# Comparing hot source numbers by tensor_tensor with a broadcast PSUM column in a gated graph layer

## The chip, the cores and the metric

The kernel runs on one core of a Trainium2 chip. The metric is the time of one execution in microseconds (us) on the device. Before the change the median of three runs is 2913.64 us (2913.59 to 2916.97).

The engines have short names here, as in the profile: PE is the matrix engine (PEld its weight load), DVE the vector engine, ACT the scalar engine, POOL is GpSimd, SP the engine that here only issues DMAs. SBUF is the on-chip memory, PSUM the smaller one that PE writes its results to.

## The reference

There are 12,500 nodes with 128 features each and 412,500 edges, sorted by their destination. Cut to what matters:

```python
theta = x[dst] - x[src]
w = sigmoid(relu(theta @ W1 + b1) @ W2 + b2)       # one gate for each edge
agg = segment_sum(w * theta, dst)
indeg = segment_sum(ones, dst)
x = layernorm(x + agg + indeg * (x @ W4 + b4))
```

So for each edge the row of its source is needed twice: through W1 for the gate, and as it is for the sum.

## The kernel before

**Tiles and stages.** First comes an opening (about 300 us): it writes a table `z` to DRAM that holds `x @ W1` and `x` for each node, keeps 8,192 of the nodes' rows in SBUF as three bfloat16 terms (`tabs`), and works on the first 18 parts of the edge list with simpler code (`early_part`). Then `part(s)` (line 1508) runs for s = 18, 19 and so on, 258 times with work of its own; two parts make a block of 104 destination nodes. Each part takes up to 1,532 edges in two kinds. Up to 1,024 *cold* edges have their source rows fetched from `z` by indirect DMA: POOL issues eight of these a part, 128 rows each (`gather`, line 404), into one of five buffers `zbuf`. Up to 512 *hot* edges have their rows picked out of `tabs` by a matrix product instead: the sources lie in 32 ranges of 256 nodes, and for each range a part has 16 hot places.

**The hot tiles.** For four ranges and up to eight parts at once, `hot_load` (line 1034) copies the hot places' source numbers, each counted from the start of its range, into `hot_src`, the same 512 half-precision numbers in every partition. `hot_tiles` (line 1046) makes two bfloat16 one-hot tiles `of` from them: partition p and tile t stand for node 2p + t of the range, and `nodes[:, t:t+1]` holds that number, so each tile is one compare on DVE (line 1052). One such fetch, two compares, falls to each part. A part later `hot_products` multiplies the tiles with `tabs` on PE (line 1068), and `hot_out` copies the rows out (line 1082, ACT). There are two `of` buffers in turn, counted by `turn_of`. In the opening five groups of such fetches (`OPENING`, line 55) fill the pipeline, 16 compares of 64 to 512 columns. Behind them 514 compares follow, 512 columns wide but for the last ones.

**What a part does on each engine.** The order on PE, DVE and ACT is written out by hand: within `part` each engine does its work in the order of the code. On DVE a part is:

- `logits` (lines 964 to 975): subtract the gathered rows from the destinations' rows `y` (964, needs the gathers), multiply (969), compare for the destination tile (939), sum up (975)
- in every other part `finish` (1237) and in the others `one_hot_h` (1154)
- `fetch_step`, which makes the two compares of line 1052
- `spend`, which does steps of placing (below)
- in every other part `normalize` (1265 to 1290)

PE in a part does the hot products with W1 (1118, 1119), then the destinations' rows of the part after next (900, into a PSUM buffer that line 964 must have read), then the hot logits (1132), the turning of hot rows (1135), and the sums of the block mixed with the products of line 1068. ACT makes one-hot tiles (879, 880), gates and scales rows (988, 1006, 1141, 1144), and copies.

**Placing.** The edge list is prepared for 64 parts at a time by the generator `place` (line 503): for each range it takes the eight largest keys, strikes them out, and flips a bit field, on DVE, with 767 columns each (lines 593, 596 and 588, with 590 in the first set). `spend` (line 1380) takes such steps as long as a part's credit lasts, 2.5 a part. So DVE has stretches with placing, in which it does these steps beside each part, and stretches without. In line 588 the other operand is a column of the PSUM tile `fix` that is broadcast along the row (`steps_c`, line 302). The tile `fix` also holds `iota_f` and `w2_b`, which lines 939, 1154 and 969 read.

**The lines that the change touches.** `fix` is carved up in lines 299 to 302; `constants` (line 324) fills the constant tiles, among them `nodes` (line 346); `hot_tiles` is in lines 1046 to 1053.

Of the kernel before, what the change touches and what calls it, by code (L numbers as in the profile page):

```python
# [14 lines left out]
AF = mybir.ActivationFunctionType  # L15
OP = mybir.AluOpType
# [4 lines left out]
P = 128  # L21
D = 128
# [4 lines left out]
WB = 104  # L27
# [19 lines left out]
HT = 2  # L47
# [7 lines left out]
OPENING = ((0,), (1, 7), (2, 6), (3, 5), (4,))  # L55
NU = 4
# [28 lines left out]
def gnn_resnorm(  # L85
# [37 lines left out]
    nc = tc.nc  # L123
# [16 lines left out]
    while n0 < N:  # L140
        t = max(1, (N - n0) // P)
# [157 lines left out]
    fix = cps.tile([P, 512], F32, name="fix")  # L299
    iota_f = fix[:, :WB].rearrange("p (o m) -> p o m", o=1)  # L300
    w2_b = fix[:, WB:WB + D]
    steps_c = fix.bitcast(I32)[:, WB + D:WB + D + HR.bit_length() - 1]
    w2_f = w2_r.rearrange("p (o m) -> p o m", o=1)

    oh_all = const.tile([P, NO * RW], F32, name="oh")
# [18 lines left out]
    def constants():  # L324

        nc.vector.tensor_copy(ident_b, ident)
        nc.vector.tensor_scalar_mul(nident_b, ident, -1.0)
        nc.vector.tensor_scalar_mul(wneg, wts[:, 0, :], -1.0)
        nc.scalar.activation(fix[:, :WB], iota_row[:, :WB], AF.Copy)

        nc.scalar.activation(w2_b, w2_r, AF.Copy)
        for k in range(HR.bit_length() - 1):
            nc.vector.memset(steps_c[:, k:k + 1], ((2 << k) - 1) << FIELD)
        half = const.tile([P, 1], F32, name="half")
        nc.vector.tensor_scalar(half, iota_p, float(HALF), -float(HALF), op0=OP.is_ge, op1=OP.mult)
        nc.vector.tensor_add(half, half, iota_p)
        nc.vector.tensor_scalar(mine, half, float(SW), None, op0=OP.is_lt)
        nc.vector.tensor_scalar(away, half, float(SW), -2.0, op0=OP.is_gt, op1=OP.mult)
        nc.vector.tensor_mul(half, half, mine)
        nc.vector.tensor_sub(away, away, half)  # L340
        nc.vector.tensor_scalar_mul(less, mine, -1.0)

        nodes = const.tile([P, HT], F32, name="nodes")
        node_c = const.tile([P, 1], F32, name="node_c")
        nc.vector.tensor_scalar(node_c, iota_p, float(HT), None, op0=OP.mult)
        nc.vector.tensor_scalar(nodes, iota_row[:, :HT], node_c, None, op0=OP.add)

        most = const.tile([P, 1], F32, name="most")
        nc.vector.memset(most, float(SW + HKL))
        apart = const.tile([P, PM], F32, name="apart")  # L350
        nc.vector.tensor_scalar(apart, iota_row[:, :PM], float(HOT), None, op0=OP.mult)
        return nodes, (apart, most)
# [14 lines left out]
    hot_src = const.tile([P, NU, RG * HB * HS], F16, name="hot_src")  # L367
# [358 lines left out]
    with tc.manual_schedule(engines={SP}), tc.tile_pool(name="work", bufs=2) as wp, tc.tile_pool(  # L726
# [312 lines left out]
        turn_of = [0]  # L1039

        def hot_of(i, x, w):

            of = of_half[i].rearrange("p (t e) -> p t e", t=HT)
            return of[:, :, x:x + w]

        def hot_tiles(f, x=0):

            i0, g, i1, i = f
            w = (i1 - i0) * HS * RG
            of = hot_of(turn_of[0] % 2, x, w)  # L1050
            for t in range(HT):
                nc.vector.tensor_scalar(of[:, t, :], hot_src[:, i % NU, :w], nodes[:, t:t + 1], None,
                                        op0=OP.is_equal)

        def hot_products(f, x, pd, steps_of):

# [264 lines left out]
        with after(done[1]):  # L1321
            place_first_dst(0, FIRST, ps_l, dst_f)
            nodes, hot_c = constants()
            start_of(0, FIRST)
# [20 lines left out]
        def tiles_of(group):  # L1345

            x = 0
            for f in group:
                hot_tiles(f, x)
                tiled.append((f, x))  # L1350
                x += (f[2] - f[0]) * EP
# [108 lines left out]
        groups, firsts, i = [], {}, 0  # L1460
# [311 lines left out]
```

## Time and profile before

| | |
|---|---|
| profiled execution | 2916.98 us |
| its span, first to last instruction | 2915.2 us |
| granted clock of PE, mean | 0.94 |
| PE busy | 2539.6 us (87%) |
| DVE busy | 2409.2 us (83%) |
| ACT busy | 2167.7 us (74%) |
| POOL busy | 2134.1 us (73%) |
| compares of line 1052 | 530, of them 502 with 512 columns |

An engine's busy time is the time in which it executes something; waiting and issuing are not counted. The page names groups by line, engine, operation, and tiles (written, then read). An entry of the waits has the engine and line that waited, what ended the wait, the total in us, how many times, and the longest. A window's row has its bounds, its length, and then the busy time and number of instructions of each engine, the granted clock, and the DMA engines' share and GB/s.

### The profile page before, as it was taken

The numbers are of one execution on the slowest core, as the hardware profiler recorded it, in microseconds if no ns is written. First come the engines' busy times: TensorE is split into PE (matmuls) and PEld (weight loads), VectorE is DVE, ScalarE is ACT, GpSimd is POOL, SyncE is SP. The second block draws the span as 40 slices with busy tenths as digits, with TensorE's granted clock in tenths as the row PEclk, the third lists the DMA queues.
The fourth block names the chain that finished last, engine by engine and source line by source line (L and its number), as shares of the span: only waits on it lengthen the run. The fifth ranks groups of instructions, "written<-read, shape, count | busy, mean of one in ns | idle before, by whom it ended". The sixth has DMA issues, their size and how long they took to land.

```text
span 2915.2 us, 59242 instructions
## 1 busy us (share of the span) xinstructions
PE 2539.6 (87%) x18606; PEld 2005.0 (69%) x18606; DVE 2409.2 (83%) x4413; ACT 2167.7 (74%) x6556; POOL 2134.1 (73%) x2213
## 2 busy tenths in 40 slices
PE   6867899999988999888888889888988899888996
PEld 6646677777776777676766667666776777666775
DVE  7888699998967999988558989988567999888664
ACT  6489877777877778677777767776776877677776
POOL 4556777777777777777777777777777777777774
PEclk8787999999999999999999999999999999999998
DMA  8544555455554555455554555555554555545542
GB/s 276 164 140 130 146 140 137 139 142 140 140 150 133 141 143 140 136 143 136 141 153 132 140 136 143 138 136 140 137 141 134 138 137 143 139 135 142 140 137 76
DMA packets 239330, 413.59 MB, mean 142 GB/s; under 512 B 63423, under 2 KB 147226, under 8 KB 237470
## 3 DMA queue, kind: packets, MB, share of 16 engines
q0 software_dynamic: 105280, 286.93, 35.4%
q1 hardware_dynamic: 131756, 116.40, 15.0%
q10 hardware_dynamic: 1970, 6.40, 0.6%
q8 instruction: 148, 2.42, 0.3%
q14 instruction: 176, 1.44, 0.2%
HBM read 388.57 MB, written 20.94 MB: 140 GB/s over the span
## 4 chain that ended last, share of the span: by engine, by line
PE 39%; ACT 22%; DVE 20%; DMA 10%; issue 8%; POOL 1%; DVEq 0%; ACTq 0%; SPq 0%; POOLq 0%
PE pa L1171 13%; DMA zbuf<-z,src_i 9%; DVE zbuf L964 6%; PE y L900 5%; PE pd L1068 5%; ACT wx L1006 4%; PE px L1132 4%; ACT wxh L1144 3%; PE pz L1118 3%; PE pz L1119 3%; PE pz L1135 3%; ACT oh L879 2%; ACT oh L880 2%; ACT xT L1082 2%; DVE ed L593 1%
## 5 line engine op out<-in xcount | busy, mean ns | idle before, releaser
L404 POOL DMA_INDIRECT zbuf<-z,src_i x2060 | 1991.3, 967 | 634.1 <-issue 247.1
L1006 ACT ACTIVATE wx<-zbuf,wx 128x128 f32<-128x128 f32 x2060 | 630.3, 388 | 0.0
L1171 PE MATMUL pa<-wx,ow 128*104 128x260 f32 (+1 forms) x2284 | 622.5, 390 | 0.0
L900 PEld LDWEIGHTS y<-y,oh 128*128 128x128 f32 (+1 forms) x2156 | 277.7, 198 | 403.1 <-DVE zbuf L964 357.5
L1068 PEld LDWEIGHTS <-tabs 128*128 128x128 bf16 x6360 | 448.9, 100 | 121.8 <-issue 5.9
L1068 PE MATMUL pd<-of,tabs 128*128 128x128 bf16 (+3 forms) x6360 | 530.7, 222 | 0.0
L1124 ACT ACTIVATE hr<-pz 128x512 f32<-128x512 f32 x258 | 152.9, 593 | 495.1 <-PE pz L1119 494.8
L900 PE MATMUL y<-y,oh 128*128 128x128 f32 (+1 forms) x2156 | 314.3, 291 | 214.1 <-DVE zbuf L964 205.3
L964 DVE TENSOR_TENSOR zbuf<-y,zbuf 128x1024 f32<-128x1024 f32 x258 | 314.9, 1220 | 166.2 <-DMA zbuf<-z,src_i 164.6
L1171 PEld LDWEIGHTS pa<-wx,ow 128*104 128x104 f32 x2284 | 338.2, 177 | 40.8
L975 DVE TENSOR_REDUCE lg<-zbuf 128x8 f32<-128x1024 f32 x273 | 329.8, 1208 | 14.1 <-ACT oh L879 0.5
L969 DVE SCALAR_TENSOR_TENSOR zbuf<-zbuf,fix 128x1024 f32<-128x1024 f32 x273 | 331.5, 1215 | 9.3
L1171 PE MATMUL pa<-wxh,owh 128*104 128x130 f32 x2064 | 326.9, 295 | 0.0
L1144 ACT ACTIVATE wxh<-pz,wxh 128x128 f32<-128x128 f32 x1032 | 294.4, 368 | 40.4 <-PE pz L1135 34.4
L1118 PE MATMUL pz<-xT,wni 128*128 128x512 f32 x516 | 279.4, 623 | 3.8 <-ACT wxh L1144 3.8
L1171 PEld LDWEIGHTS pa<-wxh,owh 128*104 128x104 f32 x2064 | 272.1, 185 | 0.0
L1132 PEld LDWEIGHTS px<-w_c,hr 128*128 128x128 f32 x2064 | 264.1, 200 | 9.9 <-ACT hr L1124 9.9
L1132 PE MATMUL px<-w_c,hr 128*128 128x1 f32 x2064 | 263.5, 249 | 7.1 <-ACT hr L1124 7.1
L1119 PE MATMUL pz<-oh,y 128*128 128x512 f32 x516 | 265.4, 596 | 1.0 <-ACT oh L880 1.0
L879 ACT ACTIVATE oh<-to_all,away,mine 128x512 f32<-128x512 bf16 (+1 forms) x257 | 213.6, 831 | 3.1 <-DMA to_all<-off_d 3.1
L1119 PEld LDWEIGHTS pz<-oh,y 128*128 128x128 f32 x516 | 98.6, 191 | 125.5 <-issue 123.7
L1135 PE MATMUL pz<-wni,xT 128*128 128x128 f32 x1032 | 176.0, 297 | 0.0
(308 smaller groups left out, 3675.9 us busy)
## 6 DMA issues: line engine op xcount, KB each, us to landing
to_all<-off_d SPq DMA_DIRECT2D x258, 128.0 KB
zbuf<-z,src_i POOLq DMA_INDIRECT x2060
hot_src<-hot_s SPq DMA_DIRECT2D x228, 128.0 KB
y<-z SPq DMA_DIRECT2D x270, 28.0 KB
xw<-in_x_dram SPq DMA_DIRECT2D x138, 52.0 KB
out_dram<-o SPq DMA_DIRECT2D x138, 52.0 KB
wx<-in_x_dram ACTq DMA_DIRECT2D x12, 512.0 KB
z<-zbuf SPq DMA_DIRECT2D x6, 1024.0 KB
```

The lines of the kernel that those rows point to most:

```text
L404: ins = nc.gpsimd.indirect_dma_start(out=rows_of(s)[:, k, :], out_offset=None, in_=z if s >= NH else x, in_offset=IndirectOffsetOnAxis(ap= ...
L900: nc.tensor.matmul(y[:, j, :], d["oh"][:, (k0 + j) * P:(k0 + j + 1) * P], y_of(s), start=True, stop=True)
L964: nc.vector.tensor_sub(half, yy.to_broadcast([P, 2, n, D]), half)
L969: nc.vector.scalar_tensor_tensor(h[:, at, :], h[:, at, :], 0.0, w2.to_broadcast([P, n, D]), op0=OP.max, op1=OP.mult)
L975: nc.vector.tensor_reduce(lg[:, at, 0], h[:, at, :], AX.X, OP.add)
L1006: weighed[0] = nc.scalar.activation(wx[:, k, :D], rows_of(s)[:, k, D:], AF.Copy, scale=wx[:, k, D:D + 1])
L1068: steps_of.append(lambda q=q, i=i, t=t, j=j: nc.tensor.matmul(to[:, q], tabs[:, g, i, q, t, :], of[:, t, q], start=j == 0, stop=j == HT * ...
L1118: nc.tensor.matmul(pz, wneg, xT, start=True, stop=False)
L1119: nc.tensor.matmul(pz, y_of(t), blocks[t // SUB]["oh"][:, BP:], start=False, stop=True)
L1132: nc.tensor.matmul(lgh()[:, t % SUB, q:q + 1], hr[:, at], w2_c, start=True, stop=True)
L1144: nc.scalar.activation(wx[:, q, :D], pz[:, q * P:(q + 1) * P], AF.Copy, scale=wx[:, q, D:D + 1])
L1171: return [lambda i=i, one=one, w=w: nc.tensor.matmul(to if len(w.shape) == 3 else to[:, 0, :], one, w, start=first and i == 0, stop=last a ...
```

## The change

A new name `nodes_c` is given to two free columns of the PSUM tile `fix`, and ACT copies `nodes` there once in the opening. In `hot_tiles` the compares of the five opening groups stay as they were: `tensor_scalar` with the node number as a per-partition scalar from SBUF. All later ones become `tensor_tensor` on DVE: the first operand is the node number's PSUM column (32-bit floats), broadcast along the row, and the second is `hot_src` (half precision, SBUF). Output and values are the same.

```diff
@@ gnn_resnorm @@
     steps_c = fix.bitcast(I32)[:, WB + D:WB + D + HR.bit_length() - 1]
+    nodes_c = fix[:, WB + D + 8:WB + D + 8 + HT]
     w2_f = w2_r.rearrange("p (o m) -> p o m", o=1)
@@ constants @@
         nc.vector.tensor_scalar(nodes, iota_row[:, :HT], node_c, None, op0=OP.add)
+        nc.scalar.activation(nodes_c, nodes, AF.Copy)
@@ hot_tiles @@
             for t in range(HT):
-                nc.vector.tensor_scalar(of[:, t, :], hot_src[:, i % NU, :w], nodes[:, t:t + 1], None,
-                                        op0=OP.is_equal)
+                if turn_of[0] < len(OPENING):
+                    nc.vector.tensor_scalar(of[:, t, :], hot_src[:, i % NU, :w], nodes[:, t:t + 1], None,
+                                            op0=OP.is_equal)
+                else:
+                    nc.vector.tensor_tensor(of[:, t, :], nodes_c[:, t:t + 1].to_broadcast([P, w]),
+                                            hot_src[:, i % NU, :w], op=OP.is_equal)
```

## The prediction

> **What bounds the kernel now.** I first read the waits over the whole run, to see who sets the pace.
>
> ```profile
> DVE zbuf L964 <- DMA zbuf<-z,src_i: 164.6, 78, 5.8
> POOL zbuf L404 <- ACT wx L1006: 141.4, 464, 0.3
> DVE px L1265 <- ACT px L1247: 90.4, 43, 5.5
> DVE a L1237 <- ACT xuT L827: 76.0, 31, 6.3
> PEld y L900 <- DVE zbuf L964: 357.5, 200, 9.7
> L404 POOL DMA_INDIRECT zbuf<-z,src_i x2060 | 1991.3, 967 | 634.1 <-issue 247.1 <-ACT wx L1006 141.4 <-DMA zbuf<-z,src_i 49.4
> L404 POOL DMA_INDIRECT zbuf<-z,src_i x2060: 940/946/1782, 269.3 to 2886.9; - x188
> ```
>
> DVE's longest total wait is for gathers (first row). POOL, which issues them, is kept by nobody: its waits, whoever is named, are never over 0.3 us. A gather takes 0.967 us, and 634.1 / 2060 = 0.308 us lie ahead of it, so 1.275 us each and 10.2 us for the eight of a part. From 269.3 to 2886.9 us POOL does nothing but this. In the long run a part cannot be shorter.
>
> But DVE is nearly full beside it, in places. The next view gives busy times of all engines; I put the bounds where stretches with placing steps begin and end, as DVE's share shows them.
>
> ```profile
> core 0: us, PE busy (x) PEld busy (x) DVE busy (x) ACT busy (x) POOL busy (x), PEclk, DMA share, GB/s
> 298.00:387.00 89.00, 74.69 (x578) 60.31 (x577) 63.04 (x120) 71.29 (x218) 67.98 (x70) 0.94 0.49 137
> 387.00:700.00 313.00, 285.41 (x2142) 225.39 (x2141) 294.90 (x512) 236.62 (x732) 238.04 (x247) 0.97 0.51 140
> 700.00:855.00 155.00, 140.65 (x1090) 111.47 (x1089) 131.56 (x240) 124.11 (x382) 117.63 (x123) 0.99 0.51 141
> 943.00:1340.00 397.00, 357.06 (x2669) 281.33 (x2668) 368.79 (x652) 300.36 (x929) 301.88 (x313) 0.96 0.51 140
> 1340.00:1502.00 162.00, 145.12 (x1099) 114.39 (x1098) 106.10 (x179) 122.44 (x377) 122.80 (x129) 0.97 0.51 140
> 1588.00:1992.00 404.00, 359.32 (x2688) 281.10 (x2686) 369.76 (x655) 300.61 (x930) 307.23 (x318) 0.97 0.51 139
> 1992.00:2157.00 165.00, 147.41 (x1082) 116.24 (x1080) 106.18 (x177) 119.62 (x373) 125.39 (x131) 0.95 0.51 139
> 2157.00:2246.00 89.00, 74.86 (x535) 61.38 (x535) 64.11 (x124) 64.38 (x197) 67.67 (x71) 0.88 0.49 134
> 2246.00:2644.00 398.00, 356.22 (x2687) 278.67 (x2686) 369.88 (x659) 300.36 (x928) 302.94 (x313) 0.97 0.52 139
> 2644.00:2840.00 196.00, 178.91 (x1300) 143.08 (x1299) 127.87 (x210) 144.13 (x445) 148.47 (x157) 0.92 0.52 140
> ```
>
> Three kinds of stretch are to be seen. In the four with placing (from 387, 943, 1588 and 2246) DVE is busy 1403.3 of 1512 us, 93%. In the light ones (from 1340, 1992, 2644) it has a third of its time free. In the four short ones between (from 298, 855, 1502, 2157; the first and last are shown) a new set is started. POOL's rate is the same in all, 0.79 gathers per us, so the heavy stretches sit where two engines are full, POOL and DVE, and PE is at 90%.
>
> **The change part by part.** *The price of a compare.* What stands now, and the nearest forms of what comes:
>
> ```profile
> L1052 DVE TENSOR_SCALAR of<-hot_src,nodes 128x512 bf16<-128x512 f16 x502 | 161.8, 364 | 6.0 <-PE pd L1068 3.1 <-DMA hot_src<-hot_s 2.9
> L939 DVE TENSOR_TENSOR ow<-fix,rel 128x416 f32<-128x416 f32 x265 | 153.8, 581 | 0.0
> L1154 DVE TENSOR_TENSOR owh<-fix,hrel 128x832 f32<-128x832 f32 x129 | 130.7, 1013 | 0.0
> L588 DVE TENSOR_TENSOR ew<-ew,fix 128x767 int32<-128x767 int32 x124 | 117.8, 950 | 2.6
> L961 DVE TENSOR_TENSOR zbuf<-y,zbuf 128x512 f32<-128x512 f32 x19 | 12.6, 682 | 3.2 <-PE y L900 3.1
> ```
>
> Lines 939 and 1154 are is_equal compares of a PSUM operand with an SBUF operand of 16 bits (`rel`, `hrel`). Between them (1013 - 581) / 416 = 1.04 ns are paid for each column, so 581 + 96 x 1.04 = 681 ns for 512 columns. Line 588, with a broadcast PSUM column as here, has 767 columns at 950 where this line gives 946; line 961 has just 512 columns at 682. All agree, so I take 681 - 364 = 317 ns more for each compare. Its bounds are 300 and 340, since neighbours overlap by some tens of ns. [...]
>
> *In the heavy stretches.* Their compares (the third has 80, too), and what DVE waited for there, for the first and the last of the four:
>
> ```profile
> 387.00:700.00 313.00, 20.62 (x64) 0.97 0.51 140
> 943.00:1340.00 397.00, 25.62 (x80) 0.96 0.51 140
> ...
> 2246.00:2644.00 398.00, 25.59 (x80) 0.97 0.52 139
> DVE a L1237 <- ACT xuT L827: 7.4, 2, 5.2
> DVE px L1265 <- ACT px L1247: 1.8, 2, 1.5
> DVE zbuf L964 <- DMA zbuf<-z,src_i: 0.2, 1, 0.2
> ...
> DVE zbuf L964 <- DMA zbuf<-z,src_i: 12.7, 9, 5.8
> DVE px L1265 <- ACT px L1247: 1.9, 2, 1.2
> DVE a L1237 <- ACT xuT L827: 1.5, 2, 1.1
> ```
>
> There are 304 compares, so 304 x 0.317 = 96.4 us more work. DVE is idle for 1512 - 1403.3 = 108.7 us, of which the lists of waits of all four stretches (two are shown) explain 64.8: 40.0 for gathers and 24.8 for ACT. The other 43.9 us are gaps too short to hold anything. If every wait vanishes, DVE needs 1403.3 + 43.9 + 96.4 = 1543.6 us, 31.6 more than the 1512 of now. If the waits for ACT stay, it is 56.4. The waits for gathers go in any case: once DVE is slower than POOL, gathers run ahead into the five buffers. The compares stand between lines 1237 and 1265, so the wait of 1265 shrinks by what they grow, while that of 1237, ahead of them, moves with PE and ACT: I take the middle, +44.
>
> *From 700 to 855* placing is still on in the first half. DVE's 23.4 idle us there are more than twice what 32 compares add (10.1): 0 to +5, I take +3.
>
> *In the four short stretches* (two a part, 16 each, 64 compares) 20.3 us are added where DVE is idle for 98. A new set passes between DVE and ACT there, so some compares lie on that path: 0 to +20, I take +5, nearest to the idle time.
>
> *In the light stretches* the cover is DVE's third of free time. There something comes back: a part waits there for the gathers now, and they will be ahead. These are the waits from 1340 and from 1992:
>
> ```profile
> DVE zbuf L964 <- DMA zbuf<-z,src_i: 39.9, 12, 5.1
> DVE zbuf L964 <- DMA zbuf<-z,src_i: 36.5, 12, 5.3
> ```
>
> PE is late next. It is busy for 145.12, 147.41 and 178.91 us. In the heavy stretch from 387, where gathers were ahead from the opening on, PE was 91.2% busy, and in the densest 100 us it was
>
> ```profile
> 1030.00:1130.00 100.00, 93.72 (x686) 74.46 (x684) 93.67 (x153) 74.60 (x231) 75.69 (x80) 0.95 0.52 141
> ```
>
> At 91.2% the three stretches shrink to 159.1, 161.6 and 196 us, 6 less together; at 93.7% to 154.9, 157.3 and 190.9, 20 less. I take the middle, -13.
>
> *Who waits for a late compare.* PE's products of line 1068 use the tiles a part later, some 8 us after they are made, and PE waited for line 1052 hardly at all; 0.6 us is covered by that. Behind the compares on DVE stand placing steps, line 1265 and the next part's line 964, for which PE's line 900 waits: that path is what the heavy term counts.
>
> *Gathers.* A compare now also lengthens gathers:
>
> ```profile
> 1641.70 0.61 DVE L1052 TENSOR_SCALAR of<-hot_src,nodes 128x512 bf16<-128x512 f16 x2
> 1641.78 1.34 POOL L404 DMA_INDIRECT zbuf<-z,src_i  x1 [0.30 <-ACT wxh L1141]
> ...
> 1007.75 0.95 DVE L588 TENSOR_TENSOR ew<-ew,fix 128x767 int32<-128x767 int32 x1
> 1007.96 0.95 POOL L404 DMA_INDIRECT zbuf<-z,src_i  x1 [0.30 <-ACT wx L1006]
> L404 POOL DMA_INDIRECT zbuf<-z,src_i x129 | 123.5, 957 | 39.3 <-issue 15.2 <-ACT wx L1006 9.4 <-DMA zbuf<-z,src_i 2.7
> ```
>
> Beside two compares of the old form a gather took 1.34 us, beside a tensor_tensor with the PSUM column the usual 0.95. All lengthening over the median is 2060 x (967 - 946) = 43 us. In the light stretch from 1340 (last row), where compares are nearly the only such operations, it is 11 ns a gather, 23 us over all. So the change frees 23 us of POOL, between 0 and 43. I count 0 of it: it pays only where POOL sets the pace, and by the sum it no longer does. [...]
>
> *The copy into PSUM* is one ACT instruction of two columns in the opening, some 0.2 us; nothing.
>
> Sum: 44 + 3 + 5 - 13 = +39 us; from its ends 31.6 + 0 + 0 - 20 = +12 to 56.4 + 5 + 20 - 6 = +75. The profiled execution took 2916.98 us (its span and 1.8 around it), so 2956 against that; the median of the runs is 3.3 us (0.1%) lower, and I forecast 2913.6 + 39 = 2953.
>
> **The rivals.** *POOL stays the bound and gets faster.* For it: gathers beside compares are longer, and DVE's waits for gathers are its largest. It decides in the heavy stretches: 64.8 us of waits hold 304 compares if one costs no more than 213 ns extra, 577 ns in all, or if ACT and PE give DVE other room. Then the time is 2914 - 23 = 2891 (2871 to 2914 by the bounds). Against it: the row with 512 columns says 682.
>
> *Two columns a cycle.* If `hot_src` and `of`, both of 16 bits, let the compare run twice as fast, it takes about 681 - 512 x 1.04 / 2 = 415 ns, 51 more than now: 15 us in the heavy stretches, all in waits, and part of the relief pays, 2914 - 15 = 2899, or nothing at all shows. Against it: lines 939 and 1154 have a 16-bit operand, too, and pay 1.04 ns a column.
>
> *Nothing hides it.* If each part is a closed ring of DVE and PE, all 514 compares count: +163, 3077. For it: PE's 357.5 us of waits for line 964. Against it: the light stretches' free DVE.
>
> *The change not doing what it says* I rule out: `turn_of` reaches five after the opening's groups, so 514 compares change form.
>
> **How the numbers follow.** The forecast has 0.70, with +12 to +75 its own range (2926 to 2989). POOL as the bound has 0.15, two columns a cycle 0.08, nothing hidden 0.07. The measurement tells 0.2%, 5.8 us, from no change. The first and last count as slower, 0.77; of the other two I put 0.17 as faster and 0.06 within 0.2%. The likeliest case's range alone leaves out over 3 in 10, so the range reaches down into the faster rival, to 2895, and up to 2989.
>
> **What would show it.** In the changed profile the compare should stand at about 680 ns with 512 columns; DVE should be over 97% busy from about 390 on in the heavy stretches, these together about 44 us longer; POOL should have waits of several us for line 1006, its buffers full; the mean gather should come nearer to 946 ns; DVE's wait for gathers should mostly be gone. I am wrong if compares stand near 420 ns, if the heavy stretches grow by far less than 30 us with POOL still never waiting, or if the light stretches grow.

## The result, and the profile after

The changed kernel takes 2960.85 us (median of five runs, 2959.41 to 2971.71) against 2913.59 us before. The ratio is 1.0169, with a 95% interval of 1.0157 to 1.0181: it is slower by 47 us. The forecast was 2953, in a range of 2895 to 2989.

The profiled execution has a span of 2961.0 us, 45.8 more than before. These lines are from its page, its groups with shapes kept apart, and its waits; they answer to those of before (lines behind the change have moved by two to six: 1052 is now 1058, 964 is 966, 404 is 406, 1237 is 1243, 1265 is 1271).

```profile
PE 2550.4 (86%) x18606; PEld 2023.8 (68%) x18606; DVE 2561.7 (87%) x4413; ACT 2165.5 (73%) x6557; POOL 2102.1 (71%) x2213
L1058 DVE TENSOR_TENSOR of<-fix,hot_src 128x512 bf16<-128x512 f32 x500 | 319.6, 680 | 2.4 <-PE pd L1074 2.4
L406 POOL DMA_INDIRECT zbuf<-z,src_i x2060 | 1957.7, 950 | 693.4 <-issue 242.5
DVE zbuf L966 <- DMA zbuf<-z,src_i: 4.8, 20, 0.6
POOL zbuf L406 <- ACT wx L1008: 197.2, 463, 5.3
DVE a L1243 <- ACT xuT L829: 124.2, 42, 7.0
DVE px L1271 <- ACT px L1253: 98.4, 38, 5.8
```

A compare of 512 columns takes 680 ns instead of 364. A gather takes 950 ns instead of 967, so POOL has 1991.3 - 1957.7 = 34 us less to do. But the two waits have changed places: DVE waits 4.8 us for gathers where it waited 164.6, and POOL, which behind the opening never waited over 0.3 us for anybody, now waits up to 5.3 us for line 1008, the last reader of a gather's buffer. POOL no longer sets the pace.

The same view of stretches as before, with bounds at the same parts of the edge list (each stretch begins where line 966 starts for the same part as line 964 did before; the prediction's bound of 700 us is 702 by this rule):

```profile
core 0: us, PE busy (x) PEld busy (x) DVE busy (x) ACT busy (x) POOL busy (x), PEclk, DMA share, GB/s
390.00:724.00 334.00, 290.93 (x2149) 230.04 (x2148) 315.73 (x516) 239.46 (x742) 244.81 (x259) 0.95 0.50 136
724.00:890.00 166.00, 146.13 (x1079) 116.50 (x1080) 139.77 (x236) 122.04 (x375) 120.48 (x128) 0.95 0.50 136
979.00:1390.00 411.00, 362.27 (x2703) 285.36 (x2700) 392.66 (x652) 299.14 (x929) 302.74 (x321) 0.96 0.50 137
1390.00:1542.00 152.00, 140.34 (x1081) 111.52 (x1080) 115.36 (x179) 120.63 (x373) 113.95 (x121) 0.98 0.52 142
1631.00:2043.00 412.00, 362.22 (x2686) 286.43 (x2684) 393.12 (x653) 299.99 (x928) 306.03 (x324) 0.95 0.50 138
2043.00:2193.00 150.00, 138.19 (x1081) 109.46 (x1080) 116.04 (x178) 119.44 (x374) 112.89 (x120) 1.00 0.53 143
2283.00:2696.00 413.00, 362.21 (x2689) 285.54 (x2687) 394.65 (x660) 299.12 (x927) 305.25 (x323) 0.96 0.50 137
```

| stretches | before, us | after, us | difference | forecast (its ends) |
|---|---|---|---|---|
| four with placing (387 to 702 before, and the three others) | 1514 | 1570 | +56 | +44 (+31.6 to +56.4) |
| behind the first of them (702 to 855 before) | 153 | 166 | +13 | +3 (0 to +5) |
| four short ones | 352 | 359 | +7 | +5 (0 to +20) |
| light ones (from 1340, 1992, and 2644 to the end) | 598 | 567 | -31 | -13 (-20 to -6) |
| opening | 298 | 299 | +1 | 0 |
| span | 2915.2 | 2961.0 | +46 | +39 |

In the heavy stretches DVE is busy for 95% (1496.2 of 1570 us) instead of 93% (1405.2 of 1514). That is 91 us more work. DVE's idle time there falls by 35 us, from 108.8 to 73.8, and the other 56 us lengthen the stretches. The light stretches are shorter than before, and the gathers of their parts are already there: DVE waited 89.0 us for them from 1340, from 1992 and from 2644, and now waits 0.6 us.

### The profile page after: what moved, and what is told of

Its sections match the earlier page's. It is cut to its first block, busy times and chain, and to the rows that moved or that the text cites. A ratio compares the mean times of both kernels' runs of the same rounds, so it can differ in the third digit from the quotient of the medians.

```text
span 2961.0 us, 59244 instructions
## 1 busy us (share of the span) xinstructions
PE 2550.4 (86%) x18606; PEld 2023.8 (68%) x18606; DVE 2561.7 (87%) x4413; ACT 2165.5 (73%) x6557; POOL 2102.1 (71%) x2213
## 4 chain that ended last, share of the span: by engine, by line
PE 40%; DVE 24%; ACT 19%; DMA 8%; issue 7%; POOL 1%; SPq 0%; DVEq 0%; ACTq 0%; POOLq 0%
PE pa L1177 13%; DMA zbuf<-z,src_i 6%; DVE zbuf L966 6%; PE y L902 5%; PE pd L1074 5%; PE px L1138 4%; ACT wx L1008 4%; PE pz L1124 3%; PE pz L1125 3%; ACT wxh L1150 3%; PE pz L1141 3%; DVE of L1058 2%; ACT oh L881 2%; DVE zbuf L971 2%; ACT oh L882 2%
## 5 line engine op out<-in xcount | busy, mean ns | idle before, releaser
L406 POOL DMA_INDIRECT zbuf<-z,src_i x2060 | 1957.7, 950 | 693.4 <-issue 242.5
L1177 PE MATMUL pa<-wx,ow 128*104 128x260 f32 (+1 forms) x2284 | 616.2, 387 | 0.0
L1177 PE MATMUL pa<-wxh,owh 128*104 128x130 f32 x2064 | 337.7, 301 | 0.0
L1058 DVE TENSOR_TENSOR of<-fix,hot_src 128x512 bf16<-128x512 f32 (+2 forms) x514 | 324.8, 673 | 2.4 <-PE pd L1074 2.4
L1177 PEld LDWEIGHTS pa<-wxh,owh 128*104 128x104 f32 x2064 | 282.4, 190 | 0.0
```

The costliest lines, as they stand in the source:

```text
L406: ins = nc.gpsimd.indirect_dma_start(out=rows_of(s)[:, k, :], out_offset=None, in_=z if s >= NH else x, in_offset=IndirectOffsetOnAxis(ap= ...
L1058: nc.vector.tensor_tensor(of[:, t, :], nodes_c[:, t:t + 1].to_broadcast([P, w]), hot_src[:, i % NU, :w], op=OP.is_equal)
L1177: return [lambda i=i, one=one, w=w: nc.tensor.matmul(to if len(w.shape) == 3 else to[:, 0, :], one, w, start=first and i == 0, stop=last a ...
```

## Experiments

All of them change the kernel after, unless said. Ratios are to the kernel before, which was run again beside each set. Two theories stood against each other. By the *full-engine* theory the longer compare costs because DVE has no free time in the placing stretches; where it has, the compare costs nothing. By the *ring* theory each part is a closed ring of waits through DVE and PE, and a longer compare delays every part by its price.

### Only in the light parts, only in the placing parts

`e1_light` takes the new form where no placing step is left, `e2_placing` where there is one:

```diff
-                if turn_of[0] < len(OPENING):
+                if turn_of[0] < len(OPENING) or steps[0] is not None:     # e1_light
+                if turn_of[0] < len(OPENING) or steps[0] is None:         # e2_placing
```

> The new form of the compare stands only in parts in which no placing step is left (about 59 of 258 parts); the rest keep the old one. Full-engine theory (the new form costs because DVE has no free time in the placing stretches): no loss, since DVE is idle for a third of the light stretches; freed gathers give 59/258 of some 30 us, so 2905 to 2914 us. Ring theory (a longer compare delays each part, placing or not): 59 x 2 x 0.317 = 37 us more, about 2951 us.

> The complement: the new form stands only in parts with placing steps left (about 199 of 258). Full-engine theory: nearly the whole loss of the full change, 2950 to 2965 us. Ring theory: 199/258 of what a closed ring would cost, and below the full change by the share of the light parts: 47 x 199/258 = 36, about 2950 us, with e1_light the missing 11 us above the kernel before. The two theories are told apart by e1_light and this one together: their differences to the kernel before add up to 47 us with both positive (ring), or this one has all of it (full engine).

Measured: `e1_light` 2909.67 us beside 2913.09 for the kernel before, ratio 0.9984 (0.9975 to 0.9994); `e2_placing` 2963.05 us, ratio 1.0183 (1.0164 to 1.0202). The 114 new compares of `e1_light` cost nothing, and even give 3 us; the 400 of `e2_placing` carry the whole loss. The ring theory asked for 2951 and 2950. It falls for the light parts: there the price is covered. `e2_placing` keeps the old compare in its light stretches, and they take 566 us, as in the changed kernel (567): that they are shorter than before (598) comes from gathers being ahead, not from the form of the compare.

### The price without the form, the form without the price

`e3_narrow` has the new form on 208 columns, as long as the old one; the other columns of the one-hot tiles are not computed. `e4_extra`, an edit of the kernel before, keeps the old form and adds a compare into a tile that nobody reads.

```diff
# e3_narrow
-                    nc.vector.tensor_tensor(of[:, t, :], nodes_c[:, t:t + 1].to_broadcast([P, w]),
-                                            hot_src[:, i % NU, :w], op=OP.is_equal)
+                    n = min(w, 208)
+                    nc.vector.tensor_tensor(of[:, t, :n], nodes_c[:, t:t + 1].to_broadcast([P, n]),
+                                            hot_src[:, i % NU, :n], op=OP.is_equal)
# e4_extra: the tensor_scalar everywhere, and behind the opening also
+                    n = min(w, 256)
+                    nc.vector.tensor_tensor(idle_of[:, :n], nodes_c[:, t:t + 1].to_broadcast([P, n]),
+                                            hot_src[:, i % NU, :n], op=OP.is_equal)
```

> The new form, but on the first 208 columns only, so that one takes about 149 + 208 x 1.04 = 365 ns, as long as the old form; the other columns of the one-hot tiles are left out and keep what stood there. DVE's time is as before, while the compare no longer lengthens gathers. Full-engine theory: POOL sets the pace again and is 20 to 34 us faster, 2880 to 2895 us. If the form itself (a PSUM operand, its place among the others) did harm beside its duration, the time would stay above 2914 us.

> The old form of the compare, and behind each one that the change touches a second compare of 256 columns from the PSUM column into a tile that nobody reads, 0.33 us of DVE time (a little more than the change adds). Full-engine theory: the old form's grip on gathers does not matter once DVE is the slower one, so the time is that of the changed kernel or up to 10 us over it, 2958 to 2972 us. If the loss came from anything but DVE's time, such as compares without the old form's width, the time would be well below 2950 us.

Measured: `e3_narrow` 2880.79 us, ratio 0.9892 (0.9875 to 0.9908); `e4_extra` 2961.3 us, ratio 1.0177 (1.0157 to 1.0196). Rows of `e3_narrow`, then of `e4_extra` (groups, and the waits of DVE for gathers and of POOL for a buffer):

```profile
L1059 DVE TENSOR_TENSOR of<-fix,hot_src 128x208 bf16<-128x208 f32 x508 | 164.6, 366 | 3.0 <-PE pd L1075 3.0
L406 POOL DMA_INDIRECT zbuf<-z,src_i x2060 | 1958.6, 951 | 634.1 <-issue 237.6 <-ACT wx L1008 141.7 <-DMA zbuf<-z,src_i 45.4
DVE zbuf L966 <- DMA zbuf<-z,src_i: 108.5, 52, 6.0
POOL zbuf L406 <- ACT wx L1008: 141.7, 465, 0.3
```

```profile
L1059 DVE TENSOR_TENSOR idle_of<-fix,hot_src 128x256 bf16<-128x256 f32 x508 | 211.5, 416 | 0.0
L1055 DVE TENSOR_SCALAR of<-hot_src,nodes 128x512 bf16<-128x512 f16 x502 | 180.8, 360 | 4.0 <-PE pd L1075 2.4 <-DMA hot_src<-hot_s 1.6
DVE zbuf L967 <- DMA zbuf<-z,src_i: 6.2, 27, 0.6
POOL zbuf L407 <- ACT wx L1009: 192.0, 473, 5.3
```

This takes the change apart. Its form alone is a gain of 32 us: at 366 ns a compare POOL, behind the opening, still never waits over 0.3 us, a gather takes 951 ns instead of 967, and 2060 x 16 ns = 33 us of pace is what the time falls by. In `e4_extra` 508 compares of 416 ns are added, 211.5 us, but they overlap their neighbours: DVE is busy 2571.7 us over the run, 162.5 us more than in the kernel before and 10 us more than in the changed kernel. DVE's time alone, with the old form, so makes the whole loss, 48 us, with the same two waits as in the changed kernel. So the loss does not come from where the operands lie.

### Three operands of 16 bits

`e5_rows16` holds 64 copies of the node number in SBUF in half precision, and reads these over and over along the row (ACT's copy into `nodes_h` in the opening is not shown):

```diff
-    nodes_c = fix[:, WB + D + 8:WB + D + 8 + HT]
+    nodes_h = const.tile([P, HT, RG * HS], F16, name="nodes_h")
@@ hot_tiles @@
-                    nc.vector.tensor_tensor(of[:, t, :], nodes_c[:, t:t + 1].to_broadcast([P, w]),
-                                            hot_src[:, i % NU, :w], op=OP.is_equal)
+                    m = w // (RG * HS)
+                    nc.vector.tensor_tensor(
+                        of[:, t, :].rearrange("p (m e) -> p m e", m=m),
+                        nodes_h[:, t, :].rearrange("p (o e) -> p o e", o=1).to_broadcast([P, m, RG * HS]),
+                        hot_src[:, i % NU, :w].rearrange("p (m e) -> p m e", m=m), op=OP.is_equal)
```

> The changed kernel with the node numbers not as a PSUM column but as 64 half-precision copies in SBUF, read over and over along the row, so that all three operands of the compare have 16 bits. The rival that fell in the changed kernel (two columns a cycle) is put to the test: if it holds here, a compare takes about 415 ns, 51 more than the old form, under the 213 ns more that the waits of the placing stretches hold; POOL sets the pace, and with gathers freed the time is 2880 to 2900 us. If it takes one column a cycle again (about 680 ns) or gathers are still lengthened, 2914 to 2965 us.

In that set of runs, and in the next, on two other chips, every kernel had a median over 4000 us, the one before included. PE's granted clock was 0.81 to 0.84 there, and PE stood idle for nothing that the profile names: in `e5_rows16` the weight loads of line 1078 have 440.1 us of such time ahead of them, where in `e5c_rows16` below they have 5.1. In `e5_rows16` a compare of 512 columns took 417 ns, 53 more than the old form. `e5_rows16` had 0.9996 (0.9952 to 1.0040), and its repetition `e5b_rows16` 1.0103 (1.0041 to 1.0164). With such runs nothing is settled, and the kernel was run a third time.

> [...] Full-engine theory: 53 ns more than the old form for 304 compares of the placing stretches is 16 us, less than the 64.8 us that DVE waits there, so POOL sets the pace, with gathers near 950 ns: 2880 to 2900 us. If this form lengthened gathers as the old one did, or if any compare slower than the old one cost time, 2914 to 2930 us.

> The kernel of e5_rows16 a third time, on a chip where the kernel before takes some 2914 us, if one is to be had. Full-engine theory: the compare costs 53 ns more than the old form, 16 us for 304 compares of the placing stretches, under the 64.8 us that DVE waits there; POOL sets the pace, with gathers near 950 ns: 2880 to 2900 us. If gathers were lengthened by this form, too, or if any slower compare cost its time, 2914 to 2930 us.

Measured: `e5c_rows16` 2927.22 us beside 2914.04 for the kernel before, ratio 1.0045 (1.0031 to 1.0059). The full-engine forecast of 2880 to 2900 missed; the other branch of the expectation holds. Groups and waits of this run, and a piece of the timeline in order of time (start and duration in us):

```profile
L1060 DVE TENSOR_TENSOR of<-nodes_h,hot_src 128x512 bf16<-128x512 f16 x500 | 188.4, 419 | 3.1 <-PE pd L1078 2.9 <-issue 0.2
L407 POOL DMA_INDIRECT zbuf<-z,src_i x2060 | 2008.0, 975 | 634.1 <-issue 227.5 <-ACT wx L1009 134.0 <-DMA zbuf<-z,src_i 55.4
DVE zbuf L967 <- DMA zbuf<-z,src_i: 161.5, 71, 6.3
POOL zbuf L407 <- ACT wx L1009: 134.0, 440, 0.3
...
1631.45 0.76 DVE L1060 TENSOR_TENSOR of<-nodes_h,hot_src 128x512 bf16<-128x512 f16 x2
1631.65 1.38 POOL L407 DMA_INDIRECT zbuf<-z,src_i  x1 [0.30 <-ACT oh L882]
```

The compare is as quick as foretold, 419 ns, and DVE has room for it: it waits 161.5 us for gathers, POOL never over 0.3. So POOL sets the pace, as in the kernel before, but a gather now takes 975 ns instead of 967. That is 2008.0 - 1991.3 = 17 us, the last gather starts 17 us later (at 2904.2 instead of 2886.9 us), and the time rose by 13. The other cause that the expectation names, a slower compare that costs its own time, would give much the same sum; but DVE still waits 26 us for gathers in the placing stretches, so it is not what holds the kernel up. My error was to think that only the old form lengthens a gather.

### Less placing in a part

`e6_after_spread` (the kernel after) and `e7_before_spread` (the kernel before) do the placing in smaller helpings:

```diff
-            credit[0] = min(credit[0] + 2.5, 5.0)
+            credit[0] = min(credit[0] + 2.35, 5.0)
```

> The changed kernel, with 2.35 instead of 2.5 units of placing allowed a part: the same placing work over about 52 parts of a set instead of 49. Full-engine theory: DVE's load in a placing part falls by some 0.2 us (6% of the 3.3 us that a placing part has more than a light one), 199 parts, 40 us less, against some 10 us for twelve more parts at the placing pace: 2925 to 2945 us. If DVE's load in placing parts did not set the pace, 2961 us stays.

> The kernel before with the same 2.35 units. There POOL sets the pace over the run, and a lighter DVE frees nothing: 2908 to 2920 us by the full-engine theory. If DVE's load in placing parts was the bound of the kernel before, too, it would fall by as much as the changed kernel does.

> [...] Full-engine theory: 2925 to 2945 us. If DVE's load in placing parts did not set the pace, 2961 us stays.

> [...] Full-engine theory: POOL sets the pace of the kernel before, so 2908 to 2920 us; if DVE's load in placing parts sets it there, too, a fall as large as that of e6b_after_spread.

The last two are the first two kernels once more. All four runs fell in the two sets with times over 4000 us. The ratios to the kernel before were 1.0092 (1.0050 to 1.0135) and 0.9953 (0.9911 to 0.9995) for the kernel after with this edit, 1.0053 (1.0007 to 1.0098) and 0.9998 (0.9952 to 1.0043) for the kernel before with it. The two sets contradict each other on the kernel after, and what bounds a kernel in them is not known. Whether smaller helpings would save the changed kernel was not settled.

### Half the price

`e8_half` gives the new form to the first compare of each fetch everywhere, to the second in light parts alone:

```diff
-                if turn_of[0] < len(OPENING):
+                if turn_of[0] < len(OPENING) or t and steps[0] is not None:
```

> Of the two compares of a fetch, the first takes the new form everywhere behind the opening, the second only in parts in which no placing step is left. In the placing stretches half the price is added: 304 x 0.317 / 2 = 48 us, against 64.8 us of DVE's waits there. Full-engine theory: the cost has a threshold; below it POOL sets the pace, and about half of its lengthening beside compares, and all in the light parts, goes: 2890 to 2910 us, faster than both kernels. Ring theory: the cost is proportional, (2961 + 2914) / 2 = 2937 us or a little less.

Measured: 2917.94 us beside 2918.33 for the kernel before, ratio 1.0005 (0.9990 to 1.0020). Over the run half the price costs nothing where the whole costs 47 us, and the ring's 2937 is out. But the gain did not come either. Its waits, one group, and its first and last heavy stretch show why:

```profile
DVE zbuf L966 <- DMA zbuf<-z,src_i: 3.0, 12, 0.6
POOL zbuf L406 <- ACT wx L1008: 134.8, 441, 0.7
DVE a L1243 <- ACT xuT L829: 132.1, 48, 8.1
L406 POOL DMA_INDIRECT zbuf<-z,src_i x2060 | 1968.5, 956 | 637.1 <-issue 237.5 <-ACT wx L1008 134.8 <-DMA zbuf<-z,src_i 48.8
388.00:710.00 322.00, 292.04 (x2149) 231.67 (x2148) 306.75 (x517) 239.30 (x743) 243.94 (x257) 0.95 0.52 140
...
2244.00:2645.00 401.00, 356.65 (x2686) 281.21 (x2684) 382.68 (x659) 300.32 (x928) 303.71 (x320) 0.97 0.52 140
```

DVE waits for gathers no more (3.0 us), and the heavy stretches are longer: 322 and 401 us against 315 and 398 for these two, 1528 against 1514 for all four. That is +14, where the whole price makes +56, so the cost is not proportional there either. DVE sets the pace in them already; that this ends just where the kernel before stands is chance: the light stretches win 26 us, as their gathers are ahead. I had put the threshold at the 64.8 us of all DVE's waits there. By these rows it lies lower. If the waits for ACT stay, as they do in the changed kernel, only the 40.0 us of waits for gathers are cover, and 48 us use them up. Where exactly it lies was not measured.

## Why the prediction was right

The sign, the mechanism and the size hold; +39 was forecast and +47 measured. That the size is so near is in part luck: two of its terms lie outside the ends given for them, and the misses partly cancel. By its steps:

- **The price of a compare.** 681 ns from the line through 416 and 832 columns; measured 680. As work of DVE the price came out a little smaller: 91 us for the 304 compares, 299 ns each, where I had 96.4 and a lower bound of 300 ns. The compares' own durations grew by 96.7 us; DVE's other instructions in these stretches were 5.4 us shorter in sum, and the overlap of neighbours stayed, at 99.6 us before and 100.0 after.
- **The heavy stretches.** Mis-sized within its ends: I took the middle, and it came out at the upper one, 56 us. The part of the step that failed is that half of the waits for ACT would be taken up. In the changed kernel the waits for gathers in the four stretches fall from 40.0 to 2.6 us, as forecast, but the waits for ACT add up to 27.2 us, where they were 24.8. For the first one:

```profile
DVE a L1243 <- ACT xuT L829: 7.2, 3, 4.4
DVE px L1271 <- ACT px L1253: 1.7, 1, 1.7
```

  Before, these were 7.4 and 1.8, and the longest of each line comes in the same part as before, some 20 us later. They did not shrink. That they move along because DVE itself lets PE and ACT begin (line 902 waits for 966) fits this, but was not tried.
- **From 702 to 855.** Forecast +3, measured +13, outside the ends I gave. I took DVE's 23.4 idle us for cover. Its waits for ACT there rose from 16.7 to 21.7 us instead of shrinking, and gathers were ahead in this stretch before the change, too (DVE waited 2.1 us for them there), so next to no wait for them could be used up. But the compares need not make all 13 us. These are the stretch before, after, and in `e4_extra`:

```profile
702.00:855.00 153.00, 138.65 (x1079) 110.47 (x1079) 129.66 (x235) 122.11 (x375) 116.11 (x121) 0.99 0.52 142
724.00:890.00 166.00, 146.13 (x1079) 116.50 (x1080) 139.77 (x236) 122.04 (x375) 120.48 (x128) 0.95 0.50 136
725.00:884.00 159.00, 139.70 (x1079) 110.58 (x1080) 139.45 (x265) 121.16 (x372) 119.18 (x126) 0.99 0.52 140
```

  `e4_extra` has the same work more on DVE, and at the granted clock of before, 0.99, it takes 6 us more. In the changed kernel the clock was 0.95, and PE was busy 7 us longer for the same number of products. How much of the 13 us goes with the clock was not separated.
- **The short stretches.** +7 against +5.
- **The light stretches.** Forecast -13, measured -31. I counted what PE's busy time would leave at 91 to 94% density. The density came out as taken, at 91 to 92%, but PE's busy time in the three stretches fell from 471.4 to 450.2 us. In the stretch from 2043 it fell from 147.4 to 138.2, and PE's granted clock was 1.00 where it had been 0.95; in the stretch from 1390 it fell from 145.1 to 140.3 at 0.98 against 0.97 (18 of 1099 products also fall outside its bounds). A fixed PE time was the wrong floor. What raised the granted clock was not tried.
- **Gathers.** I forecast 23 us freed, between 0 and 43, and none of it of use. It was 34 us, and no use: POOL waits. My reading that POOL's waits before the change are never over 0.3 us holds behind the opening alone; in the opening one lasts 14.5 us. That the gain is real where POOL sets the pace is shown by `e3_narrow`, 32 us.
- **What would show it.** The compare at 680 ns, POOL's waits for the buffers, the gather's mean, the vanished waits for gathers: all there. DVE over 97% busy was not: 95%.

The rival *POOL stays the bound* had the right mechanism and fell at the price: `e3_narrow` is this rival with the price taken away. Its limit of 213 ns extra counted the waits for ACT as room; the 40.0 us of waits for gathers alone hold 132 ns a compare, an estimate that `e8_half` fits, but does not fix. *Two columns a cycle* fell by the row of 680 ns. *Nothing hides it* fell by `e1_light`. The misses cancel in part: +12 and +10 in the placing stretches and behind the first of them, -18 in the light ones.

## What to carry to other kernels

Where two engines are both nearly full, a change that frees one and loads the other is paid by stretches, not by averages: DVE was busy 83% of the time, and still 91 us more work in its full stretches cost 56. Look in the stretch for the waits of the engine that is to get more work, and count as cover first those for the engine that will be relieved; here the waits for ACT stayed (24.8 us before, 27.2 after). And when such a trade loses, make it only where the loaded engine has room: `e1_light` does that, and at 2909.67 us (0.9984 of the kernel before, 0.9975 to 0.9994) is the only complete kernel here that is faster than both.

## What was not expected of the hardware

A tensor_tensor, too, can lengthen a gather's issue, and more than the old tensor_scalar does: beside the one with both operands in SBUF a gather took 1068 ns, beside the old form 1025. I sorted the 2060 gathers of four traces by whether a compare ran at the same time:

| compare | ns of one | gathers beside one: mean ns | other gathers: mean ns |
|---|---|---|---|
| tensor_scalar, SBUF (before) | 364 | 1025 (359) | 954 |
| tensor_tensor, PSUM column and SBUF (after) | 680 | 946 (451) | 952 |
| the same, 208 columns (`e3_narrow`) | 366 | 948 (328) | 951 |
| tensor_tensor, both from SBUF, 16 bits (`e5c_rows16`) | 419 | 1068 (362) | 955 |

The number of gathers beside a compare stands in brackets; the median of all gathers is 946 ns in each of these traces. Beside the compare with one operand in PSUM a gather is not lengthened: its mean is 946 to 948 ns. With both in SBUF it takes 122 ns more than the median, beside a compare of 419 ns, against 79 more for the old form. What makes the difference is not shown by these rows.

Also, with a row of 64 half-precision numbers that is read eight times over, tensor_tensor did 512 columns in 419 ns, as the rival *two columns a cycle* has it (415), where the broadcast PSUM column took 680. Memory, type and reading pattern changed together, so which of them does it was not separated.
